# A bidirectional scan kernel: the statistics chunks of the first six pairs, and which output product carries the bias

## The chip, the cores and the metric

One core of a Trainium2 chip runs the whole kernel; it is one launch. The metric is device time in microseconds (us) for one execution, from the start of the program to its end. Engines are written as the profile writes them: PE is TensorE with its matmuls, PEld its weight loads, DVE is VectorE, ACT is ScalarE, POOL is GpSimd, SP is SyncE, which in this kernel issues nearly all DMAs. Each engine works through its own list of instructions in order, so an instruction that waits holds up everything behind it on the same engine.

## The reference

The input x has 4 images of 128 channels and 96 x 96 points. Four sequences are made of each normalised image: along the rows (H) forward and backward, along the columns (V) forward and backward. Each goes through the same block, and the four results are put together by a last product and added to x:

```python
u, gate = in_proj(x)                     # grouped 1x1, 2 x 256 channels
u = conv5(silu(u))                       # depthwise, 5 taps
s = ssm_in(u)
a = DMIN + (DMAX - DMIN) * sigmoid(delta(u))
b, c = tanh(ssm_b(u)), tanh(ssm_c(u))
h[l] = a[l] * h[l - 1] + b[l] * s[l]     # what the cumulative sums of the reference amount to
u = u + ssm_out(c * h + d * s)
y = out_proj(mix(u * sigmoid(gate)))
x + fuse(concat(y_h, y_h_reversed, y_v, y_v_reversed))
```

The normalisation is a group norm: it needs the mean and the variance of the whole image (per group of 4 channels) before the first product of that image can use its folded weights.

## The kernel before, in words

**Phases, pairs, units.** Each image has two phases, V and then H, so there are 8. A phase has 6 steps of 16 lines, and a step 4 pairs (`R = 4`, in the order `TURN`), so a phase has 24 pairs and the kernel 192. A pair works on two units (`s` = 0 and 1), the forward and the backward direction, of 384 columns each. A pair goes through input product (`x_in` by `wn`) and SiLU, convolution (on PE for one half of the channels: matmuls on `band` and `less`; on DVE for the other half: taps at L725), copies of the convolution to `u` (L891 in the first pairs), four projections (matmuls `psum<-u,main`), the scan on DVE (L800), its output product (L556), the gating (L619), and the output product (matmuls `psum<-u,w_fin`, 16 for each unit).

**The lag.** The scan's outputs of a pair are used six pairs later (`LAG = 6`). So pairs 0 to 5 have no output part; they are written in `pair`, all others in `pair_on`, and `tail` finishes the last six. In `pair`, the DVE order is: taps of this pair, copies to `u` (L891), first work of the next pair, the scan in `recurrence`, then `stats_chunks`. The order of instructions on each engine is the order of the program text. SP issues its DMAs in program order too, and a DMA waits at the head of SP's queue until what it needs is there.

**Chunks.** While image b is in its V phase, the statistics of image b + 1 are gathered: its 24 chunks of 128 x 384 are loaded into three buffers named `xs` (`load_chunks`, DMA at L424) and each goes once through bn_stats on DVE (`stats_chunks`, L430). `chunks_of(t)` says which chunks are taken in pair t: two a pair, in the third and fourth pair of each step. `load_chunks(t + 2)`, called in pair t, asks for the chunks of pairs t + 1, t + 2 and t + 3 as far as the three buffers are free. In the first pairs that makes: pair 0 asks for chunks 0, 1, 2, pair 2 for chunk 3, pair 3 for 4 and 5, pair 4 for 6; pair 2 takes chunks 0 and 1, pair 3 takes 2 and 3, pairs 4 and 5 take none.

**Outputs.** `accumulate` makes the output product of a unit and evacuates it from PSUM to a buffer `ys` on ACT; POOL then adds `ys` into the accumulator `acc`, which holds the image itself, so the residual is in it. In the V phases both evacuations are plain copies (L835). In the H phases the output's bias `b_fin` has to be added once: the first unit of a pair (s = 0) goes through an ACTIVATE with bias (L833), the second (s = 1) through a copy. In the last pair and in `tail` some products are added straight out of PSUM by DVE (`direct`): with bias by one scalar_tensor_tensor (L850), without by a tensor_add (L852). The last loop of `tail` does the same for half products (L1135 without bias, L1137 with).

**Kinds of pairs.** In the second half of each phase's steps SiLU results are reused and no input product is needed. There a pair whose convolution needs no `less` rows (`single`, positions p = 0 and 3) has 80 matmuls between two waits in the chain, one that needs them has 96; in pairs of the first half ("fronted") the numbers are 112 or 128. In single and `less` pairs ACT runs, near the outputs: evacuation of the first product, a copy of `u` to PSUM as the seed of the scan's product (L570), evacuation of the second product; in a `less` pair another copy of `u` (L698) lies ahead of the second evacuation. Some of these pairs also compute a gate for later (L536 on PE, L574 on ACT).

**Other lines that matter.** L297 and L315 load `x_in`, L486 stores SiLU results, L657 stores edge rows, L663 loads them (`lone`), L911 stores gates.

Of the kernel before, what the change touches and what calls it, by code (L numbers as in the profile page):

```python
# [61 lines left out]
LAG = 6  # L62
# [6 lines left out]
def conv_preact_kernel(  # L69
# [55 lines left out]
    def bank(i):  # L125
        return psum[:, i, :]

    def mm(o, col, lhsT, rhs, start, stop):
        r = slice(32 * col, 32 * col + 32)
        nc.tensor.matmul(o[r, : rhs.shape[-1]], lhsT, rhs, start=start, stop=stop,  # L130
                         skip_group_check=True)
# [204 lines left out]
    b0 = phases[0][0]  # L336
# [74 lines left out]
    def chunks_of(t):  # L411

        un = units[min(2 * t, NU - 2)]
        st, k = divmod(t % NP, R)
        if un["order"] == "V" and un["b"] + 1 < B and k > 1:
            return [(un["b"] + 1, 4 * st + 2 * (k - 2) + e) for e in range(2)]
        return []

    def load_chunks(t):
        for b, c in chunks_of(t - 1) + chunks_of(t) + chunks_of(t + 1):  # L420
            if (b, c) not in loaded and len(chunks) < 3:
                loaded.add((b, c))
                chunks[b, c] = wk.tile([P, SC], F32, tag="xs", bufs=3, name=f"xs_{b}_{c}")
                nc.sync.dma_start(chunks[b, c], xr[b, :, bass.ts(c, SC)])  # L424
# [123 lines left out]
    def ssm(bi, s):  # L548

        k = bi - NU + 8 + s  # L550
        return turning[k % 3] if bi >= NU - 8 else SSM + 2 * s

    def out_of(bi, s, j):
        z = tbs[bi]
        r = slice(64 * j + 32 * s, 64 * j + 32 * s + 32)
        nc.tensor.matmul(bank(ssm(bi, s) + j)[:, :N], w_so[r, bass.ts(j, P)], z[r, :],  # L556
                         start=(bi, s) not in seeded, stop=True, skip_group_check=True)
# [7 lines left out]
    def under(bi, s):  # L565

        if bi + s == 0:
            return
        seeded.add((bi, s))
        nc.scalar.copy(psum[:, ssm(bi, s) : ssm(bi, s) + 2, :N], us[bi][:, s])  # L570
# [37 lines left out]
    def gating(bi, s):  # L608

        v = units[bi + s]["v"] = us[bi][:, s]  # L610
        m = mirror(bi // 2)
        if m is None:
            g = tile_of(bi // 2)[:, s]
        else:
            g = old_gates.get(bi // 2, tile_of(bi // 2))[:, 1 - s, :, ::-1]
        pz = psum[:, ssm(bi, s) : ssm(bi, s) + 2, :N]
        if (bi, s) not in seeded:
            nc.vector.tensor_add(pz, pz, v)
        nc.vector.scalar_tensor_tensor(v, g, 1.0, pz, ALU.add, ALU.mult)  # L619
# [161 lines left out]
    def scale_s(i):  # L781
        s = tbs[i][0:64, :]
        nc.scalar.activation(s, s, AF.Copy, scale=d_sb[0:64, 0:1])
# [29 lines left out]
    def send():  # L813
        for b, r in done:
            nc.sync.dma_start(out[b, :, r], accf[:, r])
            if b + 1 < B:
                reload.append((b + 1, r))
        done.clear()

    def accumulate(bu, bk, adder=nc.gpsimd, last=False):  # L820

        b, s, p, st = bu["b"], bu["s"], bu["p"], bu["st"]
        py = bank(bk)
        direct = last and (s == 1 or bu["order"] == "H")
        for j in range(2):
            for c in range(4):
                mm(py, c, w_fin[:, bu["dir"], j, 32 * c : 32 * c + 32], bu["v"][:, j, :],
                   j == 0, j == 1)
        y = py[:, :N]
        if not direct:  # L830
            ys = wk.tile([P, N], F32, tag="ys", bufs=4, name=f"ys_{bu['id']}")
            if s == 0 and bu["order"] == "H":
                nc.scalar.activation(ys, y, AF.Identity, bias=b_fin)  # L833
            else:
                nc.scalar.copy(ys, y)  # L835
            y = ys
        if s == 1:
            y, p, st = y[:, ::-1], R - 1 - p, NS - 1 - st
        if bu["order"] == "V":
            part = acc.rearrange("p (m q) r c -> p m q r c", q=R)[  # L840
                :, :, p, :, bass.ds(st * LN // R, LN // R)
            ]
            y = y.rearrange("p (c r m) -> p m r c", r=R, m=M)
        else:
            part = acc[:, bass.ts(st, LN), p, :]
            y = y.rearrange("p (h m) -> p h m", m=M)

        def add():
            if direct and s == 0:
                adder.scalar_tensor_tensor(part, y, b_fin, part, ALU.add, ALU.add)  # L850
            else:
                adder.tensor_add(part, y, part)  # L852
            if bu["order"] == "H" and bu["st"] >= NS // 2 and bu["end"]:

                done.extend((b, bass.ts(2 * st + e, LN * WW // 2)) for e in range(2))

        return add
# [22 lines left out]
    def pair(t):  # L880
# [15 lines left out]
        if t == 2:  # L896
            keep_lone(0)
        load_chunks(t + 2)
        proj(i, banks)
        n, s = divmod(t, 2)  # L900
# [150 lines left out]
    def tail():  # L1051

        first, end = NU // 2 - LAG, NU // 2
        wait = []

        def ssm_out(n):
            for s in range(2):
                for j in range(2):
                    out_of(2 * n, s, j)

        def z_copy(n):
            nc.scalar.copy(tbs[2 * n][64:P, :], tbs[2 * n][0:64, :])

        def gate_units(n):
            for s in range(2):
                gating(2 * n, s)
                under(2 * n + 2, s)

        def product(n, s, bk):
            if s == 0:  # L1070
                accumulate(units[2 * n], bk)()
            else:
                wait.append(accumulate(units[2 * n + 1], bk, nc.vector, True))

        def add():
            wait.pop(0)()
            send()

        z_copy(first + 1)
        ssm_out(first)  # L1080
        gate_units(first)
        adds = [accumulate(waiting.pop(0), bk) for bk in (4, 5)]
        scale_s(NU - 2)
        for part in range(2):
            scan(NU // UB - 1, part)
            outputs(2 * first + 4, None, r=bass.ts(part, N // 2))
        ssm_out(first + 1)
        outputs(2 * first + 8, None)
        for held_add in adds:
            held_add()  # L1090
        gate_units(first + 1)
        outputs(2 * first + 6, None, nc.vector)
        outputs(2 * first + 10, None)
        product(first, 0, 4)
        product(first, 1, 5)
        z_copy(first + 2)
        product(first + 1, 0, 4)
        add()
        ssm_out(first + 2)
        for n in range(first + 2, end - 1):  # L1100
            gate_units(n)
            z_copy(n + 1)
            product(n - 1, 1, 5)
            add()
            product(n, 0, 4)
            ssm_out(n + 1)
        last = 2 * (end - 1)
        half = N // 2
        for s in range(2):
            bu = units[last + s]  # L1110
            v = us[last][:, s]
            g = old_gates[last // 2][:, 1 - s, :, ::-1]
            for e in range(2):
                r = bass.ts(e, half)
                pz = psum[:, ssm(last, s) : ssm(last, s) + 2, r]
                nc.vector.scalar_tensor_tensor(v[:, :, r], g[:, :, r], 1.0, pz, ALU.add, ALU.mult)
        spots = iter((5, 4, 2, 3, 7, 6))
        for i, s, e in ((-2, 1, 0), (-1, 0, 0), (-1, 0, 1), (-2, 1, 1), (-1, 1, 0), (-1, 1, 1)):
            i += NU // 2
            bu = units[2 * i + s]  # L1120
            r = bass.ts(e, half)
            py = bank(next(spots))
            for j in range(2):
                for c in range(4):
                    mm(py, c, w_fin[:, bu["dir"], j, 32 * c : 32 * c + 32], us[2 * i][:, s, j, r],
                       j == 0, j == 1)
            y = py[:, :half]
            lines = bu["st"] * LN + e * LN // 2
            if s:
                lines = HH - lines - LN // 2  # L1130
                y = y[:, ::-1]
            part = acc[:, bass.ds(lines, LN // 2), R - 1 - bu["p"] if s else bu["p"], :]
            y = y.rearrange("p (h m) -> p h m", m=M)
            if s:
                nc.vector.tensor_add(part, y, part)  # L1135
            else:
                nc.vector.scalar_tensor_tensor(part, y, b_fin, part, ALU.add, ALU.add)  # L1137
            if bu["end"]:
                region = bass.ds(lines * WW, LN // 2 * WW)
                nc.sync.dma_start(out[bu["b"], :, region], accf[:, region])  # L1140
# [188 lines left out]
```

## Time and profile before

| what | us |
|---|---|
| timed runs | 1747.95, 1751.83, 1750.28; median 1750.28 |
| profiled execution | 1753.03 |
| its span, from first to last instruction | 1750.9 |
| outside the span | 2.1 |

The profile is of one execution. A row of a timeline reads: start (us from the start of the span), length, engine, line, operation, output<-inputs with shapes, how many such instructions were merged into the row, and in brackets how long the engine stood idle before it and what ended the wait. A row of the windows reads: the stretch, its length, busy time of PE, of its weight loads, of DVE, ACT and POOL with the number of instructions, the granted TensorE clock (1.00 is full speed), the share of time in which the DMA engines were busy, and GB/s. A row of the chain of waits reads start, length, and the work on the chain that ended last.

In this execution the projections of pairs 1 to 7 begin at 42.56, 49.37, 57.80, 67.34, 75.76, 85.52 and 95.05 us.

### The profile page before, as it was taken

How to read it: one execution, taken by the hardware profiler on the slowest of the kernel's cores; microseconds unless marked ns; L12 is line 12 of the kernel's file. 1: busy time of each engine (PE TensorE's matmuls, PEld its weight loads, DVE VectorE, ACT ScalarE, POOL GpSimd, SP SyncE). 2: the span in 40 equal slices, each digit the busy share in tenths (PEclk: the TensorE clock that was granted, in tenths of full speed). 3: DMA queues.
4: the chain of work that ended last, by engine and by line, in shares of the span. 5: the costliest groups of instructions: out<-in, count | busy, mean ns of one | idle time of the engine just before them, and what ended most of it. 6: DMA issues, size and time to landing. Idle time of an engine off the chain costs nothing.

```text
span 1750.9 us, 54410 instructions
## 1 busy us (share of the span) xinstructions
PE 1724.7 (99%) x22662; PEld 645.5 (37%) x22662; DVE 1505.8 (86%) x1508; ACT 1496.0 (85%) x2543; POOL 1454.4 (83%) x1496
## 2 busy tenths in 40 slices
PE   7999999999999999999999999999999999999998
PEld 3233333433333333334333343334333333333333
DVE  6799988888889998888889999888888888888897
ACT  4688988889888888888888888888888888888875
POOL 3488889888879988978787998898788899887886
PEclk9999999999999999999999999999999999999999
DMA  7645965358885696337897489533897549743454
GB/s 236 198 151 186 309 197 155 116 194 262 279 270 196 230 273 191 124 117 240 256 298 260 147 290 257 159 119 132 273 279 250 196 136 294 213 139 132 147 203 181
DMA packets 164980, 362.68 MB, mean 207 GB/s; under 512 B 16640, under 2 KB 128640, under 8 KB 164736
## 3 DMA queue, kind: packets, MB, share of 16 engines
q1 hardware_dynamic: 164592, 359.17, 63.6%
q8 instruction: 179, 2.93, 0.7%
q14 instruction: 65, 0.53, 0.1%
q10 hardware_dynamic: 144, 0.04, 0.0%
HBM read 220.62 MB, written 138.53 MB: 205 GB/s over the span
## 4 chain that ended last, share of the span: by engine, by line
PE 92%; DVE 2%; POOL 2%; DMA 1%; ACT 1%; issue 1%; SPq 0%; POOLq 0%; DVEq 0%; ACTq 0%
PE psum L130 78%; PE psum L556 8%; PE psum L536 5%; DMA xs<-in_xr 1%; DVE psum L725 1%; PE psum L1144 1%; DMA acc<-in_xr 0%; POOL t L806 0%; POOL t L807 0%; DVE u L619 0%; POOL acc L852 0%; POOL t L774 0%; POOL t L773 0%; SPq L486 0%; ACT psum L570 0%
## 5 line engine op out<-in xcount | busy, mean ns | idle before, releaser
L725 DVE SCALAR_TENSOR_TENSOR psum<-sil,small,psum 128x768 f32<-128x768 f32 x576 | 589.1, 1023 | 41.4 <-ACT psum L723 16.7
L130 PE MATMUL psum<-u,w_fin 128*32 128x384 f32 (+1 forms) x6192 | 541.6, 484 | 1.0 <-ACT ys L833 0.5
L130 PE MATMUL psum<-u,main 128*32 128x384 f32 x6144 | 536.8, 490 | 2.3 <-DVE u L891 2.3
L619 DVE SCALAR_TENSOR_TENSOR u<-gate,psum 128x768 f32<-128x768 f32 x376 | 341.9, 951 | 158.2 <-ACT ys L835 59.8
L852 POOL TENSOR_TENSOR acc<-ys,acc 128x384 f32<-128x384 f32 x375 | 427.3, 1161 | 18.6 <-DMA acc<-in_xr 4.9
L806 POOL TENSOR_TENSOR t<-t,t 64x384 f32<-64x384 f32 (+1 forms) x192 | 275.6, 1435 | 70.7 <-DVE t L800 53.5
L130 PEld LDWEIGHTS psum<-u,w_fin 128*32 128x32 f32 x6192 | 195.7, 110 | 308.9 <-issue 237.9
L570 ACT COPY psum<-u 128x768 f32<-128x768 f32 x383 | 300.3, 799 | 10.4 <-DVE u L619 4.4
L130 PEld LDWEIGHTS psum<-u,main 128*32 128x32 f32 x6144 | 180.4, 110 | 327.3 <-issue 217.2
L130 PE MATMUL psum<-sil,band 128*32 128x384 f32 x3072 | 286.5, 490 | 1.1 <-ACT gate L580 1.1
L773 POOL TENSOR_SCALAR t<-tm 64x384 f32<-64x384 f32 x184 | 173.6, 943 | 117.4 <-ACT tm L762 105.4
L807 POOL TENSOR_TENSOR t<-t,t 64x384 f32<-64x384 f32 (+1 forms) x192 | 234.0, 1219 | 15.1
L723 ACT ACTIVATE psum<-sil,small 128x768 f32<-128x768 f32 x191 | 172.5, 903 | 73.4 <-DVE u L619 64.8
L774 POOL TENSOR_TENSOR t<-t,tm 64x384 f32<-64x384 f32 x192 | 210.5, 1096 | 28.6 <-ACT t L765 13.9
L556 PE MATMUL psum<-t,main 32*128 32x384 f32 x1536 | 226.9, 526 | 3.2 <-ACT psum L570 2.6
L725 DVE SCALAR_TENSOR_TENSOR u<-sil,small,psum 128x768 f32<-128x768 f32 x192 | 194.9, 1015 | 6.8
L506 ACT ACTIVATE sil<-psum,bnorm 128x385 f32<-128x385 f32 x384 | 192.0, 585 | 5.0 <-PE psum L130 2.9
L536 PE MATMUL psum<-x_in,wn 32*128 32x384 f32 x768 | 162.1, 498 | 0.0
L130 PEld LDWEIGHTS psum<-sil,band 128*32 128x32 f32 x3072 | 88.7, 108 | 173.5 <-issue 63.1
L835 ACT COPY ys<-psum 128x384 f32<-128x384 f32 x281 | 129.3, 477 | 21.7 <-PE psum L130 19.0
L762 ACT ACTIVATE tm<-psum,small 128x384 f32<-128x384 f32 x192 | 111.1, 579 | 15.7 <-PE psum L130 6.5
L574 ACT ACTIVATE gate<-psum,bnorm 128x384 f32<-128x384 f32 x152 | 88.0, 581 | 39.8 <-PE psum L536 23.4
(109 smaller groups left out, 1529.6 us busy)
## 6 DMA issues: line engine op xcount, KB each, us to landing
gate<-kept SPq DMA_DIRECT2D x114, 768.0 KB, 5.9
kept<-gate SPq DMA_DIRECT2D x74, 768.0 KB, 3.7
sil<-sil SPq DMA_DIRECT2D x64, 770.0 KB, 7.5
lone<-edge SPq DMA_DIRECT2D x39, 770.0 KB, 7.7
x_in<-in_xs SPq DMA_DIRECT2D x250, 96.2 KB, 3.4
edge<-sil SPq DMA_DIRECT2D x96, 192.5 KB, 4.3
out<-acc SPq DMA_DIRECT2D x48, 384.0 KB, 6.1
acc<-in_xr SPq DMA_DIRECT2D x39, 384.0 KB, 6.8
```

The lines of the kernel that those rows point to most:

```text
L130: nc.tensor.matmul(o[r, : rhs.shape[-1]], lhsT, rhs, start=start, stop=stop, skip_group_check=True)
L506: nc.scalar.activation(sils[step][:, s, j, g, :], bank(bk)[:, : N + 1], AF.Silu, bias=bn[:, 1:2] if j else bn[:, 4 + g : 5 + g],)
L536: nc.tensor.matmul(bank(to)[:, :N], stats[un["b"]][0][r, s, :], x_in[s][r, q, off : off + N], start=True, stop=True)
L556: nc.tensor.matmul(bank(ssm(bi, s) + j)[:, :N], w_so[r, bass.ts(j, P)], z[r, :], start=(bi, s) not in seeded, stop=True, skip_group_check= ...
L570: nc.scalar.copy(psum[:, ssm(bi, s) : ssm(bi, s) + 2, :N], us[bi][:, s])
L619: nc.vector.scalar_tensor_tensor(v, g, 1.0, pz, ALU.add, ALU.mult)
L725: nc.vector.scalar_tensor_tensor(us[i][:, :, 1, :] if k == K - 1 else part, src, w_tap[:, k : k + 1], part, ALU.mult, ALU.add,)
L773: nc.gpsimd.tensor_scalar(*decay(i))
L774: nc.gpsimd.tensor_mul(ta[0:64, p, :], tb[0:64, :], tm[0:64, :])
L806: engine.tensor_mul(ta[0:64, p, r], tb[64:P, r], ta[64:P, p, r])
L807: engine.tensor_add(tb[0:64, r], ta[0:64, p, r], tb[0:64, r])
L852: adder.tensor_add(part, y, part)
```

## The change

Part A touches the first six pairs. `chunks_of(t)` now gives one chunk a pair for t = 2, 3, 4, 5 (chunk t - 2) and none for t = 0 and 1; and as long as the pair asked for is no later than `LAG + 1`, `load_chunks(t)` asks only for the chunks of that pair, not for those of its neighbours. So pairs 0 to 3 ask for chunks 0 to 3, one each, pair 4 for chunks 4 and 5, pair 5 for 6 and, from pair 6 on, everything is asked and taken as before.

Part B swaps the roles of the two units in the H phases: the copy goes with s = 0 and the ACTIVATE with bias with s = 1; the direct adds are swapped likewise. The number of instructions of each kind on ACT stays the same but for a few in the tail.

```diff
@@ chunks_of
         st, k = divmod(t % NP, R)
+        if t < LAG:
+            return [(b0 + 1, t - 2)] if t > 1 else []
         if un["order"] == "V" and un["b"] + 1 < B and k > 1:
             return [(un["b"] + 1, 4 * st + 2 * (k - 2) + e) for e in range(2)]
         return []
 
     def load_chunks(t):
-        for b, c in chunks_of(t - 1) + chunks_of(t) + chunks_of(t + 1):
+        ahead = chunks_of(t - 1) + chunks_of(t) + chunks_of(t + 1)
+        for b, c in ahead if t > LAG + 1 else chunks_of(t):
             if (b, c) not in loaded and len(chunks) < 3:
@@ accumulate
-            if s == 0 and bu["order"] == "H":
+            if s == 1 and bu["order"] == "H":
                 nc.scalar.activation(ys, y, AF.Identity, bias=b_fin)
             else:
                 nc.scalar.copy(ys, y)
@@ accumulate, add
-            if direct and s == 0:
+            if direct and s == 1 and bu["order"] == "H":
                 adder.scalar_tensor_tensor(part, y, b_fin, part, ALU.add, ALU.add)
             else:
                 adder.tensor_add(part, y, part)
@@ tail
-            if s:
+            if s == 0:
                 nc.vector.tensor_add(part, y, part)
             else:
                 nc.vector.scalar_tensor_tensor(part, y, b_fin, part, ALU.add, ALU.add)
```

## The prediction

> **What bounds the kernel now.** I read the page first, then a view of the stretch between the first pairs and the tail, then the first pairs engine by engine.
>
> ```profile
> PE 1724.7 (99%) x22662; PEld 645.5 (37%) x22662; DVE 1505.8 (86%) x1508; ACT 1496.0 (85%) x2543; POOL 1454.4 (83%) x1496
> PE 92%; DVE 2%; POOL 2%; DMA 1%; ACT 1%; issue 1%; SPq 0%; POOLq 0%; DVEq 0%; ACTq 0%
> 95.00:1670.00 1575.00, 1573.85 (x20776) 587.90 (x20776) 1374.19 (x1333) 1389.83 (x2359) 1350.46 (x1367) 1.00 0.64 208
> ```
>
> PE is busy for 99% of the span, and it makes 92% of the chain that ended last. Between 95 and 1670 us (third row: length, then busy time of PE, weight loads, DVE, ACT, POOL, granted clock) it is idle for 1575.00 - 1573.85 = 1.15 us. So work taken off another engine there is worth nothing unless PE's own pairs get shorter, and whatever is won before 95 us is carried unchanged to the end. The gaps that can be won lie in pairs 2 to 6. VectorE (DVE) first, then PE:
>
> ```profile
> 52.16 1.03 DVE L430 BATCH_NORM_STATS2 bn<-xs 128x6 f32<-128x384 f32 x2 [2.54 <-DMA xs<-in_xr]
> 58.12 0.55 DVE L430 BATCH_NORM_STATS2 bn<-xs 128x6 f32<-128x384 f32 x1
> 62.11 0.56 DVE L430 BATCH_NORM_STATS2 bn<-xs 128x6 f32<-128x384 f32 x1 [3.43 <-DMA xs<-in_xr]
> 62.58 3.19 DVE L725 SCALAR_TENSOR_TENSOR psum<-sil,small,psum 128x768 f32<-128x768 f32 x3
> 66.74 1.02 DVE L891 COPY u<-psum 128x384 f32<-128x384 f32 x2
> 67.78 1.75 DVE L800 TENSOR_TENSOR_SCAN t<-t 64x768 f32<-64x768 f32 x1
> ```
>
> ```profile
> 57.80 2.79 PE L130 MATMUL psum<-u,main 128*32 128x384 f32 x32 [1.62 <-DVE u L891]
> 63.99 0.88 PE L130 MATMUL psum<-x_in,wn 32*32 32x385 f32 x16 [0.32 <-DMA x_in<-in_xs]
> 65.69 0.99 PE L130 MATMUL psum<-x_in,wn 32*32 32x385 f32 x16 [0.82 <-DMA x_in<-in_xs]
> 67.34 4.45 PE L130 MATMUL psum<-u,main 128*32 128x384 f32 x32 [0.66 <-DVE u L891]
> 75.76 2.79 PE L130 MATMUL psum<-u,main 128*32 128x384 f32 x32
> ```
>
> DVE stands still twice in front of a bn_stats whose chunk has not landed (2.54 and 3.43 us); behind it in DVE's order stand the taps of the next pair (L725) and the copies (L891) without which PE can't start that pair's projections (the matmuls psum<-u,main). PE waits 1.62 us for them in pair 3 and 0.66 in pair 4, and 0.32 + 0.82 for x_in. The projections of pair 4 take 4.45 us in place of 2.79, for a reason that the windows show (same columns as above):
>
> ```profile
> 64.90:68.30 3.40, 1.95 (x28) 0.73 (x32) 3.33 (x5) 1.45 (x3) 0.00 (x0) 1.00 0.91 242
> 68.30:71.70 3.40, 3.40 (x24) 0.87 (x16) 3.30 (x4) 1.96 (x4) 0.43 (x1) 0.50 0.98 343
> 82.00:85.40 3.40, 3.40 (x24) 0.87 (x16) 1.33 (x3) 2.01 (x4) 3.25 (x4) 0.50 0.44 175
> ```
>
> In two stretches of 3.40 us the granted clock is 0.50, and each costs half its length, 1.70 (for the first 4.45 - 2.79 = 1.66 is seen directly). That makes 3.4 us beside the waits.
>
> **Part A, the chunks.** Number and kind of bn_stats stay: chunks 0 and 1 were taken in pair 2, 2 and 3 in pair 3; now 0, 1, 2, 3 are taken in pairs 2, 3, 4, 5. Of SyncE's DMAs three chunk loads were issued together in pair 0; now one goes in each of pairs 0 to 3.
>
> ```profile
> 38.66 4.31 SPq L424 DMA_DIRECT2D xs<-in_xr  x3
> 49.26 2.39 SPq L297 DMA_DIRECT2D x_in<-in_xs  x2
> 58.71 0.38 SPq L424 DMA_DIRECT2D xs<-in_xr  x1
> 59.79 2.90 SPq L297 DMA_DIRECT2D x_in<-in_xs  x4
> DMA to landing us min/median/max: 2.3/4.7/13.5
> ```
>
> Step 1, the first wait. Chunk 0 is still asked at 38.66 behind the same transfers, so I leave the 2.54 us. But pair 2 then takes one chunk, not two: half of 1.03, 0.5 us, goes from in front of the taps of pair 3. PE's wait of 1.62 shrinks by that, and the projections of pair 3 start at 57.3 instead of 57.80.
>
> Step 2, the second wait. Chunk 1 is asked in pair 1, beside its x_in loads at 49.26; with the median landing of 4.7 it is there at 54, with twice that at 58.5, and it is wanted at 57.6 (now 58.12, less 0.5). So the 3.43 us go, to within 0.9. The taps of pair 4 begin near 58.2 instead of 62.58, 4.4 us earlier, and DVE no longer sets pair 4. Chunks 2 and 3 are asked nearly two pairs ahead of use too, with the same margin.
>
> Step 3, what is late next. The x_in loads: PE's second group of x_in matmuls waited until 65.69 and ends at 66.68. If those loads land when they did, pair 4's projections start at 66.68 instead of 67.34: 0.66 won. SP now reaches its four loads at 59.79 with fewer waits ahead; as the group waits 0.32 and 0.82 only for landing, the most to win besides is their sum, 1.1. Nearest is the middle of these ends, since one chunk load less (0.38 of SP's time) is ahead and the DMA engines are 0.91 busy there: 1.2 us, with bounds of 0.66 and 1.8.
>
> Step 4, the added bn_stats in pairs 4 and 5, 0.55 each. DVE's copies were at 66.74 and PE's projections follow 0.6 later. From one pair's copies to the next pair's DVE has copies, scan, three taps and the last tap, 1.02 + 1.75 + 3.19 + some 1.0 = 7.0 us of work, 7.5 with one bn_stats. Without half clock pair 4 takes PE 75.76 - 67.34 - 1.66 = 6.76. After the change DVE's copies of pair 4 come when PE's convolution allows it, near 63.5, so it has some 2.5 us in hand against the projections at 66.1, and the 0.7 that it falls behind in pair 4 stays covered. If that cover is gone, the cost is 0.7.
>
> Step 5, the half clock. With the first stretch gone pair 5 starts 1.2 + 1.66 = 2.9 earlier, with the second gone too pair 6 starts 4.6 earlier; if both come again, 1.2 stays. Nothing here shows that a shorter wait takes a stretch away: the one at 68.30 follows a window with PE at 1.95 of 3.40, which the change would fill; for the second I see no such cause. I take the middle, one of the two: A is worth 2.9 (0.7 to 5.2).
>
> The Trainium skill, page "TensorE: Matmul & The Clock Gate", Part 1 (What's actually happening), says that the clock falls to half after an idle activity window of about 3.4 us and that the windows run free, without regard to the kernel's start. The trace agrees on the length (3.40) and not on the condition, as PE was busy for 1.95 us ahead of the first stretch. By the rule's condition neither kernel would have such a stretch in these pairs, and A would be worth 1.2; by its free-running windows the stretch would fall elsewhere in each execution, which is the first rival below.
>
> **Part B, the bias.** In the pairs of the H phases ACT's ACTIVATE with bias now evacuates the second output product, the plain COPY the first. ACT's sum doesn't change. Both kinds are in the trace, as the V phases use COPY for both. First an H single pair, then a V one:
>
> ```profile
> 330.69 0.59 ACT L833 ACTIVATE ys<-psum,b_fin 128x384 f32<-128x384 f32 x1 [0.17 <-PE psum L130]
> 331.17 0.81 ACT L570 COPY psum<-u 128x768 f32<-128x768 f32 x1
> 331.98 0.48 ACT L835 COPY ys<-psum 128x384 f32<-128x384 f32 x1
> ```
>
> ```profile
> 118.72 0.48 ACT L835 COPY ys<-psum 128x384 f32<-128x384 f32 x1 [0.17 <-PE psum L130]
> 119.10 0.81 ACT L570 COPY psum<-u 128x768 f32<-128x768 f32 x1
> 120.01 0.48 ACT L835 COPY ys<-psum 128x384 f32<-128x384 f32 x1
> ```
>
> The seed of the scan's product (L570), for which PE's next matmuls wait, starts 0.48 after an ACTIVATE and 0.38 after a COPY. The chain of waits shows that this reaches PE (start of a piece, its length):
>
> ```profile
> 113.34 6.60 PE psum L130 x80
> 129.88 7.53 PE psum L130 x96
> 325.31 6.61 PE psum L130 x80
> 342.05 7.53 PE psum L130 x96
> ...
> 1649.29 7.53 PE psum L130 x96
> ```
>
> Two single pairs take 129.88 - 113.34 = 16.54 in V and 342.05 - 325.31 = 16.74 in H: 0.10 a pair. In the H phases there are 22 such pairs (six in each of the first three, four in the last), so 2.2 us are to be won. Against it: the second copy now ends later. In a V single pair it begins 1.29 after the first; with the ACTIVATE in second place its end moves from 1.77 to 1.87. In the pairs that take the `less` rows in the middle (x96, 23 in the H phases) the weight loads stand close behind it:
>
> ```profile
> 349.64 0.48 ACT L835 COPY ys<-psum 128x384 f32<-128x384 f32 x1 [0.22 <-PE psum L130]
> 349.94 0.41 PEld L536 LDWEIGHTS psum<-x_in,wn 32*128 32x128 f32 x3
> 350.26 0.20 PEld L536 LDWEIGHTS psum<-x_in,wn 32*128 32x128 f32 x3
> 351.08 0.16 PEld L130 LDWEIGHTS psum<-u,main 128*32 128x32 f32 x8 [0.62 <-ACT gate L574]
> ```
>
> Three loads that take 0.20 elsewhere take 0.41 there, so the last of them begins near 350.17, right after the copy's end at 350.12: it waits for it. 0.10 later is at most 0.10 x 23 = 2.3 us lost, at least nothing, as the next projections wait for ACT's L574 in any case. Nearest is the low end, a quarter: 0.6. Part B: 2.2 - 0.6 = 1.6 won, between 2.2 won and 2.3 lost (the singles' gain eaten by their own second copy).
>
> The tail swaps a few ACTIVATEs for COPYs and STTs for adds:
>
> ```profile
> 1728.24 1.50 PE L130 MATMUL psum<-u,w_fin 128*32 128x384 f32 x16 [0.46 <-ACT ys L833]
> L833 ACT ACTIVATE ys<-psum,b_fin x94: 568/581/587, 305.4 to 1740.9; 128x384 f32<-128x384 f32 x94
> ```
>
> PE waits 0.46 there for the ACTIVATE of a first product, which becomes a COPY and 0.10 shorter; the few direct adds of second products gain the bias and lie on the same path. I put the two against each other: 0, with 0.5 either way (the first row's wait). The second row gives the number of ACTIVATEs in the H phases and the tail, 94, which rival 4 needs.
>
> **Sum.** 2.9 + 1.6 = 4.5 us. The profiled execution took 1753.03 (span 1750.9 and 2.1 outside it), so it would become 1748.5. The timed runs have a median of 1750.28, 2.75 below; whether they held both half-clock stretches (3.4 us) I can't see. If neither kernel's timed runs hold any, A is worth 1.2 there, and with one stretch saved 2.9. I take a value between, nearer to the second, since this profile is the one execution that I see: A is 2.3 against the median: 1750.28 - 2.3 - 1.6 = 1746.4.
>
> **Rivals.**
> 1. The half clock comes again, or as much of it elsewhere. For it: two stretches in the profile, of which the second follows no long wait. Against: the first follows the longest wait that the change removes. A is 1.2: 1750.28 - 1.2 - 1.6 = 1747.5.
> 2. B gives back in the `less` pairs what it wins in the singles. For it: the load at 350.17. Against: L574 in front of the next projections. 1750.28 - 2.3 = 1748.0.
> 3. Part A doesn't do what it says: a chunk asked one pair at a time lands late, or the x_in loads take the wait's place in full. For it: landings up to 13.5 us, and x_in waits of 0.32 and 0.82 already there. Against: the median of 4.7. A is 0 to 0.7, so 1750.28 - 0.4 - 1.6 = 1748.3.
> 4. Slower: the second evacuation, and not the first, frees the bank that PE needs in every pair, and the ACTIVATE puts 0.10 on PE's path in each. It decides as soon as nothing else ends later than that copy, as at 350.12. The price is 0.10 x 94 = 9.4 (94 ACTIVATEs in H phases), without the singles' 2.2: 1750.28 - 2.3 + 9.4 = 1757.4; in half of the pairs 1752.7. Against: in most pairs matmuls of another kind lie between.
>
> **How the numbers follow.** The forecast has 0.50, rivals 1 to 4 have 0.16, 0.13, 0.11 and 0.10. About 0.2%, 3.5 us, is what a measurement of this kernel can tell from no change, so faster means under 1746.8. The forecast lies just past that edge; I give it seven in ten to be measured as faster (0.35), and a third of the 0.40 of rivals 1 to 3, which lie 0.7 to 1.5 on the other side of it (0.14): together 0.50. Slower (over 1753.8) has most of rival 4, 0.08, and 0.42 is left for no change. The range runs from A at its most, 1750.28 - 5.2 - 1.6 = 1743.5, to rivals 2 and 3 with half of what the three timed runs lie under their median (1750.28 - 1747.95 = 2.3), 1748.3 + 1.2 = 1749.5; rival 4 is left out with its 0.10.
>
> **What would show it.** Right: no DVE wait for xs in pair 3 (one near 2.5 in pair 2 stays); projections of pair 4 at 65.5 to 66.7, of pair 5 at 72.5 to 75; two H singles at 16.54. Wrong: an x_in wait above 1 us in pair 4, a bn_stats that waits in pairs 3 to 5, `less` pairs in H longer by 0.1, fronted pairs in H longer than in V, half clock at 0.50 in more windows than two.

## The result and the profile after

| | before | after |
|---|---|---|
| timed runs, median (us) | 1750.09 (15 runs, 1747.79 to 1753.38) | 1746.77 (15 runs, 1744.72 to 1749.81) |
| ratio after to before | | 0.9979, 95% interval 0.9971 to 0.9987 |
| profiled execution, and its span | 1753.03, 1750.9 | 1749.81, 1747.9 |

By the medians the change wins 3.3 us; by the ratio it wins 0.21%, 3.7 us, and the interval lies wholly under 1, from 2.3 to 5.1 us. The profiled execution after is the slowest of its 15 runs, so I read its start first. Page, then windows (length; busy time of PE, weight loads, DVE, ACT, POOL; granted clock; DMA share; GB/s):

```profile
PE 1725.2 (99%) x22662; PEld 649.8 (37%) x22662; DVE 1506.3 (86%) x1508; ACT 1495.2 (86%) x2543; POOL 1451.6 (83%) x1496
PE 94%; DVE 2%; DMA 1%; ACT 1%; POOL 1%; issue 1%; SPq 0%; DVEq 0%; POOLq 0%; ACTq 0%
```

```profile
23.80:27.20 3.40, 3.09 (x66) 1.70 (x63) 0.41 (x6) 2.47 (x6) 0.00 (x0) 0.80 0.26 77
27.20:30.60 3.40, 3.40 (x46) 1.35 (x29) 0.12 (x2) 3.14 (x7) 0.00 (x0) 0.50 0.30 71
30.60:34.00 3.40, 3.40 (x24) 3.18 (x31) 0.70 (x2) 0.65 (x2) 1.53 (x2) 0.50 0.27 79
34.00:37.40 3.40, 3.40 (x40) 0.87 (x44) 3.01 (x7) 1.71 (x4) 1.59 (x3) 0.50 0.23 57
37.40:40.80 3.40, 3.40 (x38) 1.10 (x30) 2.93 (x4) 0.82 (x2) 0.00 (x0) 0.69 0.52 162
95.00:1670.00 1575.00, 1574.85 (x20808) 591.82 (x20800) 1377.43 (x1335) 1391.29 (x2364) 1351.08 (x1370) 1.00 0.65 208
```

The bound is the same: PE is idle for 0.15 us of the 1575. But the clock was halved for 13.7 us at the start (counting the first and the last window by their share), before the first pair and so before anything that the change touches. The projections of pair 0 begin at 42.17, against 35.68 before. In spite of that pair 6 begins at 85.02, against 85.52. DVE and PE in between:

```profile
55.90 0.55 DVE L433 BATCH_NORM_STATS2 bn<-xs 128x6 f32<-128x384 f32 x1
56.37 3.12 DVE L728 SCALAR_TENSOR_TENSOR psum<-sil,small,psum 128x768 f32<-128x768 f32 x3
62.66 0.55 DVE L433 BATCH_NORM_STATS2 bn<-xs 128x6 f32<-128x384 f32 x1
71.23 0.56 DVE L433 BATCH_NORM_STATS2 bn<-xs 128x6 f32<-128x384 f32 x1
78.69 0.56 DVE L433 BATCH_NORM_STATS2 bn<-xs 128x6 f32<-128x384 f32 x1
```

```profile
42.17 2.79 PE L130 MATMUL psum<-u,main 128*32 128x384 f32 x32
...
62.44 2.79 PE L130 MATMUL psum<-u,main 128*32 128x384 f32 x32
...
69.17 2.79 PE L130 MATMUL psum<-u,main 128*32 128x384 f32 x32
...
76.40 2.79 PE L130 MATMUL psum<-u,main 128*32 128x384 f32 x32 [0.40 <-DVE u L894]
```

One bn_stats a pair, none of them with a wait in brackets: both waits of before are gone. That for chunk 0 went with the slow start: SP asked for it 0.3 us after the projections of pair 0 began, and 3.0 us after in the second profile below, so here it had more time to land. Lines are three higher than before (L430 is L433, L891 is L894, L725 is L728). All projections take 2.79, none 4.45. A second profile of the same kernel, from a run without the slow start, shows what is usual (DVE, then PE):

```profile
51.81 0.56 DVE L433 BATCH_NORM_STATS2 bn<-xs 128x6 f32<-128x384 f32 x1 [1.63 <-DMA xs<-in_xr]
52.28 3.12 DVE L728 SCALAR_TENSOR_TENSOR psum<-sil,small,psum 128x768 f32<-128x768 f32 x3
...
57.30 0.55 DVE L433 BATCH_NORM_STATS2 bn<-xs 128x6 f32<-128x384 f32 x1
57.77 1.00 DVE L728 SCALAR_TENSOR_TENSOR psum<-sil,small,psum 128x768 f32<-128x768 f32 x1
59.34 2.08 DVE L728 SCALAR_TENSOR_TENSOR psum<-sil,small,psum 128x768 f32<-128x768 f32 x2 [0.57 <-ACT sil L509]
```

```profile
56.98 2.79 PE L130 MATMUL psum<-u,main 128*32 128x384 f32 x32 [0.28 <-DVE u L894]
...
63.08 0.88 PE L130 MATMUL psum<-x_in,wn 32*32 32x385 f32 x16 [0.23 <-DMA x_in<-in_xs]
64.60 0.88 PE L130 MATMUL psum<-x_in,wn 32*32 32x385 f32 x16 [0.65 <-ACT sil L509]
65.41 2.79 PE L130 MATMUL psum<-u,main 128*32 128x384 f32 x32
...
72.17 2.79 PE L130 MATMUL psum<-u,main 128*32 128x384 f32 x32
```

The wait for chunk 0 stays (1.63), that for the chunk in pair 3 is gone. What is late next is x_in, in both groups of its matmuls. The profile puts the wait of the second group, 0.65, down to ACT's SiLU (L509), but PE doesn't need that SiLU: in the kernel before the same matmuls ran at 65.69, and ACT's SiLUs of that pair began only at 67.70. Here are SP's four loads in the second profile, and then ACT's row of the kernel before:

```profile
59.07 2.50 SPq L297 DMA_DIRECT2D x_in<-in_xs  x4
```

```profile
67.70 1.98 ACT L506 ACTIVATE sil<-psum,bnorm 128x385 f32<-128x385 f32 x4
```

SP is through with the loads at 61.57, and PE goes on 3.03 us later; in the kernel before it is 62.69 and 3.00 us. In the trace the last x_in landing that these matmuls wait for comes at 64.47, 0.13 ahead of them, as at 65.55 before (0.14). The SiLU that is named merely ended in between.

In the H phases, the single pair on ACT, and four pairs of the chain of waits of after (start, length):

```profile
330.40 0.48 ACT L838 COPY ys<-psum 128x384 f32<-128x384 f32 x1 [0.17 <-PE psum L130]
330.77 0.81 ACT L573 COPY psum<-u 128x768 f32<-128x768 f32 x1
331.69 0.58 ACT L836 ACTIVATE ys<-psum,b_fin 128x384 f32<-128x384 f32 x1
```

```profile
325.04 6.59 PE psum L130 x80
...
333.30 6.59 PE psum L130 x80
...
341.56 7.53 PE psum L130 x96
...
350.69 7.53 PE psum L130 x96
...
359.90 6.59 PE psum L130 x80
```

and of the same chain of before the two rows that were not shown yet:

```profile
351.09 7.60 PE psum L130 x96
360.25 6.61 PE psum L130 x80
```

Two singles take 341.56 - 325.04 = 16.52 where they took 16.74; the two `less` pairs behind them take 359.90 - 341.56 = 18.34 where they took 360.25 - 342.05 = 18.20. So 0.22 is won and 0.14 given back.

### The profile page after: what moved, and what is told of

The parts are those of the page before. It is cut to its first block, busy times and chain, and to the rows that moved or that the text cites. A ratio compares the mean times of both kernels' runs of the same rounds, so it can differ in the third digit from the quotient of the medians.

```text
span 1747.9 us, 54407 instructions
## 1 busy us (share of the span) xinstructions
PE 1725.2 (99%) x22662; PEld 649.8 (37%) x22662; DVE 1506.3 (86%) x1508; ACT 1495.2 (86%) x2543; POOL 1451.6 (83%) x1496
## 4 chain that ended last, share of the span: by engine, by line
PE 94%; DVE 2%; DMA 1%; ACT 1%; POOL 1%; issue 1%; SPq 0%; DVEq 0%; POOLq 0%; ACTq 0%
PE psum L130 80%; PE psum L559 8%; PE psum L539 6%; DVE psum L728 1%; DMA x_in<-in_xs 1%; DVE u L622 0%; DMA acc<-in_xr 0%; ACT psum L726 0%; POOL t L809 0%; DVE u L728 0%; PE psum L1162 0%; POOL t L810 0%; DVE t L803 0%; ACT psum L573 0%; POOL t L777 0%
## 5 line engine op out<-in xcount | busy, mean ns | idle before, releaser
L728 DVE SCALAR_TENSOR_TENSOR psum<-sil,small,psum 128x768 f32<-128x768 f32 x576 | 589.0, 1023 | 45.6 <-ACT psum L726 20.6
L855 POOL TENSOR_TENSOR acc<-ys,acc 128x384 f32<-128x384 f32 x375 | 419.5, 1140 | 17.4 <-DMA xs<-in_xr 3.9
L777 POOL TENSOR_TENSOR t<-t,tm 64x384 f32<-64x384 f32 x192 | 210.1, 1094 | 28.4 <-ACT t L768 13.7
L509 ACT ACTIVATE sil<-psum,bnorm 128x385 f32<-128x385 f32 x384 | 192.1, 583 | 10.5 <-PE psum L130 7.8
L728 DVE SCALAR_TENSOR_TENSOR u<-sil,small,psum 128x768 f32<-128x768 f32 x192 | 194.9, 1015 | 6.8
L559 PEld LDWEIGHTS psum<-t,main 32*128 32x128 f32 x1536 | 94.6, 183 | 75.7 <-issue 42.5
```

Source lines behind the costliest of these rows:

```text
L509: nc.scalar.activation(sils[step][:, s, j, g, :], bank(bk)[:, : N + 1], AF.Silu, bias=bn[:, 1:2] if j else bn[:, 4 + g : 5 + g],)
L728: nc.vector.scalar_tensor_tensor(us[i][:, :, 1, :] if k == K - 1 else part, src, w_tap[:, k : k + 1], part, ALU.mult, ALU.add,)
L777: nc.gpsimd.tensor_mul(ta[0:64, p, :], tb[0:64, :], tm[0:64, :])
```

## The experiments

To compare kernels I use two things: the timed ratio to the kernel before, and from the profile the time from the projections of pair 0 to those of pair 8 (part A lies in it) and from pair 8 to pair 186 (part B lies in it). This takes the start out.

| kernel | ratio, 95% interval | pair 0 to 4 | 0 to 8 | 8 to 186 | half clock in pairs 3 to 5 |
|---|---|---|---|---|---|
| before | | 31.66 | 68.50 | 1570.7 | two stretches |
| before, again | one run | 31.58 | 65.95 | 1569.8 | one |
| B alone | 1.0000 (0.9990 to 1.0011) | 30.54 | 64.91 | 1568.6 | none |
| asks apart | 1.0003 (0.9992 to 1.0013) | 31.06 | 65.44 | 1569.3 | none |
| takes one | 0.9994 (0.9982 to 1.0005) | 29.91 | 65.77 | 1569.1 | one |
| A alone | 0.9983 (0.9971 to 0.9995) | 28.61 | 62.82 | 1569.9 | none |
| A with sides | 0.9973 (0.9960 to 0.9986) | 29.29 | 63.52 | 1567.9 | none |
| A with singles | 0.9970 (0.9958 to 0.9982) | 27.32 | 61.74 | 1566.7 | none |
| after | 0.9979 (0.9971 to 0.9987) | 27.00 | 61.67 | 1567.9 | none |
| after, again | 0.9975 (0.9965 to 0.9984) | 29.17 | 63.37 | 1568.5 | none |
| late | 0.9983 (0.9971 to 0.9996) | 27.13 | 62.00 | 1569.4 | none |
| late with sides | 0.9970 (0.9959 to 0.9982) | 27.15 | 62.02 | 1568.9 | none |
| late with sides, again | 0.9966 (0.9954 to 0.9978) | 27.64 | 62.50 | 1568.1 | none |

**Before, again.**

> The kernel before once more, for a second profile. Theory (the two half-clock stretches in pairs 4 and 5 and the single waits of 0.7 near pair 71 and 1.0 near pair 113 belong to that one execution and not to the kernel): from the projections of pair 0 to those of pair 8 about 65.2 us in place of 68.50, and from pair 8 to pair 186 at most 1569.8 in place of 1570.7. Rival (they belong to the kernel's own order of work): 68.5 and 1570.7 again.

0 to 8 is 65.95 with one stretch of half clock, so two stretches are not fixed in the kernel; 1569.8 says the same of the single waits further on. The theory holds but for the one stretch. DVE, PE, and the windows there:

```profile
52.04 1.19 DVE L430 BATCH_NORM_STATS2 bn<-xs 128x6 f32<-128x384 f32 x2 [2.82 <-DMA xs<-in_xr]
61.63 0.56 DVE L430 BATCH_NORM_STATS2 bn<-xs 128x6 f32<-128x384 f32 x1 [2.91 <-DMA xs<-in_xr]
```

```profile
57.84 4.46 PE L130 MATMUL psum<-u,main 128*32 128x384 f32 x32 [2.10 <-DVE u L891]
```

```profile
54.40:57.80 3.40, 1.35 (x48) 0.31 (x32) 3.33 (x5) 0.44 (x1) 1.01 (x1) 1.00 0.95 329
57.80:61.20 3.40, 3.35 (x24) 1.14 (x28) 0.92 (x2) 2.38 (x5) 0.00 (x0) 0.51 0.88 239
```

The two statistics waits come again, and the stretch again follows a long wait of PE, here in pair 3 and not in pair 4.

**A alone and B alone.** Each is the diff with the hunks of the other left out.

> Part A without part B. Theory (A takes the statistics waits out of pairs 2 to 4 and is the larger part of the change, B is a small net gain): 2.0 to 3.0 us under the kernel before, about 1747.5, with no wait of DVE for xs in pairs 3 to 5, and single pairs in H still 8.36, less pairs still 9.11. Rival (the gain comes from B, and what the first pairs take is set by the half clock that strikes somewhere anyway): within 1 us of the kernel before.

0.9983 is 3.0 us, at the upper end of what the theory named; 0 to 8 is 62.82, and up to 100 us DVE waits for xs in pair 2 alone, by 0.30. A is the larger part of the change.

> Part B without part A. Theory: in each H phase six pair lengths fall by 0.10 (two of them by 0.075) and six others grow by 0.03 to 0.09, net 0.2 a phase, 0.85 in all: 0.5 to 1.2 us under the kernel before, waits in pairs 2 to 4 as before. Rival: B carries the whole difference, 3 us. A second rival: it carries none, 0.

The ratio, 1.0000, can't tell 0.85 us from nothing; its interval excludes 3. The profile does tell, by the mean length of pairs at the same place in the four H phases (from projections to projections, before and after):

| place in the phase | kind | before | after |
|---|---|---|---|
| 9, 10, 13, 14 | singles | 8.36 | 8.26 |
| 17, 18 | singles | 8.31, 8.30 | 8.24, 8.23 |
| 7, 8 | less | 9.12, 9.11 | 9.16, 9.20 |
| 11, 12 | less | 9.11, 9.11 | 9.14, 9.20 |
| 15, 16 | less | 9.11, 8.93 | 9.14, 9.00 |

B alone has the numbers of after to 0.01. In one phase the singles win 4 x 0.10 + 2 x 0.075 = 0.55 and the others lose 0.34; over four phases 2.2 won, 1.35 lost, 0.85 net. Fronted pairs don't move.

**A with singles.** The bias goes with the second product in single pairs alone. The kernel adds the bias twice in some parts of the image and not at all in others, because a unit with s = 1 lies mirrored; the work per pair is the same.

```diff
-            if s == 0 and bu["order"] == "H":
+            if bu["order"] == "H" and s == bias_at[0]:
...
+            bias_at[0] = 1 if single and not fronted else 0
             if n:
                 add = accumulate(waiting.pop(0), bk, *adder)
```

> Part A, and of part B only the single pairs without an input product (the first product goes by COPY, the second has the bias there; in all other pairs the bias stays with the first product as before). Theory: it keeps the 2.2 us of the singles (22 x 0.10) and drops what the less pairs lose (about 1.35 in four phases), so 1.2 to 1.4 us under the changed kernel and 4.3 to 5 under the kernel before; less pairs in H at 9.11, singles at 8.26. Rival (the loss in the less pairs belongs to the swap in the singles ahead of them, the second copy there being late): less pairs stay longer by 0.03 to 0.09, and the time is that of the changed kernel.

0.9970, with the `less` pairs at 9.12 and 9.11 again and the singles at 8.26. So the loss belongs to the `less` pairs' own second evacuation and not to the singles ahead of them. That this is the wait of the third weight load, the rows of after show (ACT and weight loads):

```profile
349.15 0.58 ACT L836 ACTIVATE ys<-psum,b_fin 128x384 f32<-128x384 f32 x1 [0.32 <-PE psum L130]
349.77 0.31 PEld L539 LDWEIGHTS psum<-x_in,wn 32*128 32x128 f32 x4
350.62 0.16 PEld L130 LDWEIGHTS psum<-u,main 128*32 128x32 f32 x8 [0.55 <-ACT gate L577]
```

The ACTIVATE ends at 349.73; only two loads go before it, and the rest stand as a group of four from 349.77 (before it was three and three, the third waiting within its group).

**A with sides, late, late with sides.** In "sides" ten units of each of the first three H phases carry the bias with s = 1: the five evacuated in single pairs (3, 4, 7, 8, 11) and their mirrored ones, so that each place has it once. In "late" the first four chunks are not taken in the first six pairs at all:

```diff
+        if t < LAG:
+            return []
...
+            extra = {6: 0, 7: 1, 10: 2, 11: 3}
+            more = [(b0 + 1, extra[t])] if t in extra else []
-            return [(un["b"] + 1, 4 * st + 2 * (k - 2) + e) for e in range(2)]
+            return more + [(un["b"] + 1, 4 * st + 2 * (k - 2) + e) for e in range(2)]
```

> Part A with the same partial swap as the kernel above. Theory: 1.4 us under part A alone (1744.3 where part A alone was 1745.7), 0.5 to 0.7 under the changed kernel; in H 8.26 for the singles, 9.11 for the less pairs, fronted pairs unchanged to 0.01. Rival: equal to part A alone.

0.9973 against 0.9983 of A alone is 1.7 us, with intervals that overlap; 8 to 186 falls from 1569.9 to 1567.9.

> Without part B; the first four chunks of image 1 are not taken in the first six pairs at all but as a third chunk in pairs 6, 7, 10 and 11, where PE has more to do. Theory (bn_stats and its chunk cost only where DVE or a landing sets the pair, which is in pairs 2 to 5): at least the gain of part A alone, and up to 1.5 us more where the wait for chunk 0 in pair 2 was left, so 2.5 to 4 us under the kernel before. Rival (from pair 6 on DVE has no room for a third chunk, or three loads at once come late): pairs 6, 7, 10 and 11 grow by up to 0.5 each and the time is 0.5 to 2 us over part A alone.

From pair 0 to 4 it is 27.13 against 28.61 of A alone. All of that lies from pair 3 to pair 4 (6.74 against 8.23), and chunk 0 is not the reason, as A alone waited 0.30 for it and lost nothing by that: with no chunk load ahead of them SP is through with its four x_in loads at 59.03 and not at 60.83, and PE's wait of 0.74 in pair 4 is gone. From pair 5 to 8 it is 28.11 against 27.44, as the third chunk lengthens pairs 6 and 7: nearly half of the win is given back. The ratio is that of A alone.

> The first four chunks of image 1 taken as a third chunk in pairs 6, 7, 10 and 11, as in the run before; and of the bias swap only ten units of each of the first three H phases: the five that are evacuated in single pairs and gain, and the five mirrored ones, evacuated in fronted pairs, that must go with them so that each part of the image has the bias once. Theory: the 2.2 to 3.8 us of the late chunks and 3 x (4 x 0.10 + 0.075) = 1.4 us of the singles add up, without a loss in the less pairs: 1744 when the kernel before is at 1749.2, under the changed kernel by 1 to 2. Rival (the mirrored units cost in the fronted pairs what the singles gain): fronted pairs in H longer by 0.05 to 0.10, time that of the late chunks alone.

0.9970, and again:

> The late chunks with the partial swap once more, on the same chip as the changed kernel. Theory: 0.5 to 2 us faster than the changed kernel (0.8 in the first pairs, 0.5 from the less pairs that lose nothing), 0.9967 to 0.9975 of the kernel before. Rival: no difference from the changed kernel.

0.9966 on a chip where the changed kernel has 0.9975: 1.6 us between the two, as expected (the ratio itself is a hair past the 0.9967 to 0.9975 that was named), and the intervals overlap. The fronted pairs keep their length to 0.01 but for one place. It is the fastest of the kernels with the reference's whole computation; that it beats the changed one is likely by these numbers, not settled.

**Takes one and asks apart.** The two halves of part A. In the first, chunks are taken one a pair and asked for by the old rule; in the second they are taken as before and asked for two, one, one.

> Half of part A: one chunk taken in each of pairs 2 to 5, but asked for by the old rule (pair 0 asks two, pairs 1 and 2 one each, pair 3 two, as far as the buffers are free), so two loads in pair 0 in place of one. Theory (what counts is when a chunk is needed, not when it is asked): no wait of DVE for xs beyond that for chunk 0, 2 to 3 us under the kernel before, equal to part A alone within 0.7. Rival (two loads at once share the DMA engines with the SiLU stores, and the first lands late): a wait for xs in pair 2 of over 1 us and 1 us or more over part A alone.

```profile
51.88 0.56 DVE L432 BATCH_NORM_STATS2 bn<-xs 128x6 f32<-128x384 f32 x1 [2.20 <-DMA xs<-in_xr]
57.38 0.55 DVE L432 BATCH_NORM_STATS2 bn<-xs 128x6 f32<-128x384 f32 x1
```

```profile
65.65 4.44 PE L130 MATMUL psum<-u,main 128*32 128x384 f32 x32
```

The first row is DVE's wait in pair 2, 2.20 against 1.63 in the changed kernel; the wait in pair 3 is gone as the theory says. But the time is 0.9994, not 0.9983, so the theory is likely wrong that asking is of no account; the two intervals overlap (0.9982 to 1.0005, 0.9971 to 0.9995), so it is not settled. A stretch of half clock hit this profile too (4.44), so of 65.77 some 1.7 is that.

> The other half: chunks taken as before (two in pair 2, two in pair 3, none in pairs 4 and 5), but asked two in pair 0, one in pair 1, one in pair 2, so that the third no longer queues in pair 0 and the fourth follows as soon as its buffer is free. Theory (the fourth chunk can't be asked until pair 2 has let go a buffer, and is wanted 9 us later at the end of pair 3): the wait of about 3.4 us in pair 3 stays, and the time is within 0.7 us of the kernel before. Rival (the long wait was due to three loads at once): the wait is under 1.5 us, and the time 1.5 us or more under the kernel before.

```profile
51.74 1.16 DVE L432 BATCH_NORM_STATS2 bn<-xs 128x6 f32<-128x384 f32 x2 [2.04 <-DMA xs<-in_xr]
61.58 0.56 DVE L432 BATCH_NORM_STATS2 bn<-xs 128x6 f32<-128x384 f32 x1 [3.19 <-DMA xs<-in_xr]
```

The long wait stays, 3.19, and the time is 1.0003. So it was not the three loads at once that made it. What is left is the theory, that the fourth chunk had no buffer until pair 2 let one go; a fourth buffer was not tried.

**After, again.**

> The changed kernel once more. Theory (A wins some 2 us in pairs 2 to 5 with a start like that of the kernel before; its first profile started 6 us later under half clock and thereby lost the wait for chunk 0): a start with the projections of pair 0 near 36, from there to pair 8 62.5 to 63.7 us, a wait of DVE for xs in pair 2 only, and 0.9977 to 0.9983 of the kernel before. Rival (61.7 us and no wait for xs are the kernel's own): the same 61.7 with an early start.

Pair 0 starts at 36.24, pair 8 comes 63.37 later, up to 100 us DVE waits for xs in pair 2 alone, and the ratio is 0.9975.

## Why the prediction was right, point by point

Forecast were 1746.4 us, 2.3 from A and 1.6 from B; measured were 1746.77 against 1750.09.

Step 1 held: the wait for chunk 0 stayed (1.63 in the second profile, 0.30 with A alone; 2.54 had been assumed), and the projections of pair 3 came at 56.98, forecast 57.3. Step 2 held: no wait of DVE for xs in pairs 3 to 5, and the taps of pair 4 at 57.77, forecast 58.2. (Twice the median landing gives 58.7 there and not 58.5, so the margin was 1.1; nothing changes by it.) Step 3 held in its mechanism: what is late next is x_in, with 0.23 and 0.65, and pair 4's projections came at 65.41 (forecast 66.1, bounds 65.5 to 66.7). Step 4 held in the second profile, where pair 5 at 72.17 has no wait for DVE; in the first it waits 0.40 for DVE's copies (the row at 76.40), within the 0.7 that was named.

These times are from the start of the span, and the second profile began 0.56 later than the one that the forecast was worked out from. Counted from pair 0, pair 4 came after 29.17 us (forecast 30.4, bounds 29.8 to 31.0) and pair 5 after 35.93 (36.8 to 39.3 had been named as the sign). So the size of steps 1 to 3 was too small, by 1.2 us in this profile. Two signs that had been named as wrong came near: the `less` pairs grew by 0.03 to 0.09 (named was 0.1), and the first profile has half clock in four windows, though at the start.

Step 5, the half clock, was the uncertain one. Profiles without any half clock in these pairs give A's worth without it: 64.91 and 65.44 with the old taking of chunks, 62.82, 63.52 and 63.37 with A and a usual start, so 65.2 - 63.2 = 2.0. The prediction put 1.2 on that case; the term was too small, since pair 4 starts 1.2 to 2.4 earlier there (28.61 to 29.29 from pair 0, against 30.54 and 31.06) and pair 5 another 0.2.

Stretches of half clock showed in these pairs in three of the five profiles in which chunks are taken or asked for by the old rule, and in none of the eight others (A in full, or the late chunks). Two of the four stretches followed waits for DVE's copies behind a late chunk (2.10; and 0.66, next to 0.82 for x_in). The one in takes one followed waits of 0.41 and 0.63 for x_in, about what the changed kernel still has (0.23 and 0.65), and one followed next to no wait. What the four share is little work of the array in the 3.41 us ahead, which the last section shows. By that measure, laid over every possible position of the 3.41 us windows, a stretch in pairs 2 to 5 would come in 0.65 and 0.58 of the executions of B alone and asks apart, and in 0.14, 0.14 and 0.38 of those of A alone, the changed kernel's second profile and A with sides: an estimate of some 0.4 stretches, 0.7 us, that A saves. The timed runs say about the same: their granted clock has a mean of 0.9986 over 85 runs of the kernel before and of 0.9991 over 25 of the changed one, and the difference, 0.00055 of 1750 us, is 1.0 us. The prediction had 1.1 for it (2.3 - 1.2), as a middle between two values and not from a cause, so that this term came out is luck in part. Rival 1 fell by its time: it put A at 1.2, and A has 2.0 without any half clock.

Part B: the singles' 2.2 came as worked out. The loss in the `less` pairs is the term that was mis-sized: 0.6 had been taken, "nearest is the low end, a quarter", of the 2.3 at most; it is 1.35. The reason given, that the projections wait for ACT's gate (L574) in any case, did not cover it: that gate waits itself for the matmuls whose weights were late. Net 0.85 and not 1.6; rival 2 (all given back) was about as near as the forecast. The timed runs alone can't tell it from nothing (B alone, 1.0000). Rival 4 fell: no fronted pair is longer. Rival 3 fell with A alone. The tail took 76.11 us from pair 186, 76.03 before: 0.1, forecast 0 with 0.5.

So 2.0 + 0.85 = 2.9 from the profiles, with 0.7 to 1.0 for the half clock 3.6 to 3.9, stands beside 3.7 (2.3 to 5.1) from the first ratio and 0.0025 x 1750.3 = 4.4 (2.8 to 6.1) from the second. The forecast's total, 3.9, was near because A was taken too small (2.3, against 2.7 to 3.0) and B too large (1.6, against 0.85): the mechanisms were right, and that the sizes made up for each other is luck.

## What to carry to other kernels

When a small periodic job waits for its data in front of the bounding engine's feeder, look at how many buffers it takes from in one go: two a pair with three buffers meant that the fourth load was asked for only when it was needed (asked at 58.71 in the kernel before, and wanted when the bn_stats at 58.12 was done). Taking one a pair removed that wait, and the whole gain showed only with asking one a pair as well. Look also at what stands behind such a load in the DMA queue: here x_in was late next. Where two evacuations free banks for different consumers, the slower one costs in whichever position its consumer stands right behind it, and kinds of pairs can differ in that; read the pair lengths by place, for the total hides 2.2 won and 1.35 lost. Before you believe a releaser that a profile names, see whether another run did the same work without it. And take the start out before two profiles are compared: here it differed by 6.5 us.

## What the runs showed of the hardware

The granted clock fell to 0.50 for 13.7 us at the start of two of the 13 profiles (after, and A with singles), with PE busy 3.09 and 3.40 of 3.40 us in the rows above; the projections of pair 0 began at 42.17 and 43.15 in place of 34.9 to 36.3 in the others, and both executions were among the slowest of their kernels (1749.81 and 1749.41). Inside the pairs it came in single stretches of 3.41 us, and the share of PE's busy time ahead of them doesn't tell when. In the windows just ahead of the four stretches PE was busy for 1.31 (before, again), 1.96 (before), 2.37 (takes one) and 3.26 us (before, ahead of 82.00); but after 54.65:58.06 in the kernel before, with 1.79 us, the clock stayed at 1.00.

In each of the five profiles that have such stretches, all of them begin on one grid of 3.413 us, on which the fall of the clock at the end of the span lies too; in the kernel before the two stretches are four steps apart (68.31 and 81.97). That end gives the grid of the other profiles. What tells the windows of the grid apart is the array's work: for each matmul the moving columns, times the share of the 128 x 128 array that its tile covers. The window ahead of 82.00 shows it (kernel before):

```profile
78.48 0.92 PE L536 MATMUL psum<-x_in,wn 32*128 32x384 f32 x4
79.32 2.35 PE L130 MATMUL psum<-x_in,wn 32*32 32x385 f32 x32
81.60 2.48 PE L130 MATMUL psum<-sil,band 128*32 128x384 f32 x16
```

The first row is 4 x 384 / 4 = 384 columns of the whole array and the second 32 x 385 / 16 = 770; with the part of the third that lies in the window it is 1391, though PE is busy for 3.26 us. The projections do 32 x 384 / 4 = 3072 in 2.79 us. Ahead of the other three stretches it is 1054, 1358 and 1402, ahead of the two slow starts 1297 and 1478, where much of PE's time goes to 32 x 32 tiles of x_in. Within these starts, at half clock, it stays at 1290 to 1438 for three windows, which fits that the stretch there is four windows long. The lowest windows without half clock behind them have 1519 (B alone, 61.4) and 1528 (the kernel before, the 54.65 above). The 13 profiles have 6590 windows of the grid from 12 us on. Each of the 25 with at most 1478 is followed by half clock (13 of them at the end of the span, as PE runs out of work), and none of the 6565 others, which have 1519 or more. Only in the first 12 us, as PE's work begins, are there windows with less and a clock of 1.00. So the traces fall into two kinds by this number; no run set the work of a window alone.

The Trainium skill, "TensorE: Matmul & The Clock Gate", Part 1 (What's actually happening), has free-running windows of about this length, by which the same waits may or may not cost a stretch. The grid of 3.413 us, which lies at another place in each execution, agrees with that. Its condition, an idle window, is not what these rows show, as PE was busy for 38 to 96% of the windows ahead.
